# A graph-attention kernel: its set-up's key products in 13 bursts over six PSUM banks

## The chip, the core and the metric

The kernel runs on one core of a Trainium2 chip. The metric is the device time of one execution in microseconds (us); lower is better. A core has a matrix engine (TensorE, PE in the profile; its weight loads are PEld), a vector engine (DVE), a scalar engine (ACT), GpSimd (POOL) and SyncE (SP, which mostly issues DMAs). Each engine works through its own list of instructions in order and waits on semaphores for the others. Matrix products land in PSUM, which has eight banks of 128 partitions by 512 f32; everything else lies in SBUF or in device memory.

## The reference

A layer of graph attention with 16 batches of N = 512 nodes and F = 512 features, 16 heads of 32 features, and only the first 20 nodes as keys. It is done in two directions `d`: the mask with 11 labels, and its transpose. In short:

```
self_feat = concat(x, where(x.sum(-1) == 0, 0, cond)) @ W_self.T + b_self
output = self_feat
for d in range(2):
    A = (mask if d == 0 else mask.swapaxes(1, 2))[:, :, :20]    # B x N x 20 x 11 labels
    kv = self_feat[:, :20]
    q = (self_feat @ Wq[d].T + bq[d]) in 16 heads;  k = (kv @ Wk[d].T + bk[d]) in 16 heads
    aff = q . k / sqrt(32)                                      # B x N x 16 x 20
    aff = where(A.sum(-1) > 0, aff, NEG) + A @ w_bias + b_bias
    w = softmax(aff, over the 20 keys)
    output += (w @ kv) @ Wout[d] + bout[d]                      # per head
return x + relu(output)
```

## The kernel before

**What is kept and what is folded.** A score q·k is linear in the node's feature vector, so the kernel never forms q. The set-up folds each key through Wq once, and a batch's scores are then products of 512-long feature vectors with these folded keys. A softmax doesn't change if the first key's score is taken from all, so 19 key differences (`ND`) are folded in place of 20 keys. In all 16 batches x 19 differences = 304 columns per direction and head, over 512 features. The loop over batches behind the set-up forms the large products from fewer ones by sums and differences of blocks (`x_sum`, `feat_sum`, `key_sum`; `product`, line 257, forms the node features by seven such products per batch).

**The set-up, line 697 on.** In its order on PE:

- Six matmuls on a block of ones (line 735), while the first loads are on their way.
- `kv_terms` (line 780): the features of the 20 key nodes of all batches, with the part from `cond`. DVE forms from them `kvD`, the 19 differences of each batch.
- `key_rows` (line 832): Wk times `kvD`, for direction d and a group of four heads, into a PSUM bank; `key_end` puts the result into SBUF as `khD`, on whose partitions lie the four heads of 32 features each.
- **The key bursts**, `keys` (line 929). They form Wq times `khD`. The contraction is over 32 features of one head, so a matmul takes only 32 rows of PE, and the four heads of a group (`hl` = 0 to 3) are issued one after the other on the four row groups and run side by side. The output has 128 features (chunk `fc`) by the run's columns. There are 16 stages (fc, hg) with two directions each. The unit of the plan is one batch's 19 columns: 20 bursts take 25 or 26 units, 475 or 494 columns for each head, and a burst that crosses the end of a direction or a stage is cut into two runs. Heads 0 and 1 go to one pair of PSUM banks (tag `s0`), heads 2 and 3 to the other (`s1`). In the trace the two pairs appear under names that end in 0 and 1, as `s_g(2, 0, 0, 0, 16)0_776`.
- After each burst its results are copied with the softmax's scale into a stage's tile `st` in SBUF: heads 0 and 1 by ACT (line 960), heads 2 and 3 by DVE (line 962), one copy per run. When a stage is full, GpSimd copies the part of batches 0 and 1 into `gg` (line 965) and SP stores the rest, 1064 KB, to device memory `g_d` (line 968), from which the main loop loads it batch by batch. Three of the four head groups take their tiles from a pool of three (`setup_g`, line 868), the last from a pool of their own (`late`); a tile is written again only when its store has landed.

**Fillers.** The four banks of `s0` and `s1` can be written again only when ACT and DVE have copied them. So that PE has work until then, other matmuls of the set-up stand between the bursts. They take turns over four rotating accumulator banks (tag `acc`, pool `ps_acc`, line 697). What stands after which burst is the string `plan` (line 990), one letter for each step from the lists at line 981:

- k: `key_rows` (before the plan's first entry); m: `bias_terms`, DVE only (line 856); b: `biases`, ACT and DVE
- v and w: `values` (line 892), the 20 key nodes' features times Wout, a quarter of the contraction at a time. `value_pieces` adds the bias on DVE (line 917) and stores the blocks.
- c: `bias_scores` (line 870), the query bias's scores with the keys. ACT copies them, GpSimd adds `b_bias`, four DMAs store them to `cq_d`.
- n: `row_flags` (line 217), which nodes of x sum to something other than zero
- p: `block_product` (line 971), the seven feature products of batch 0 (line 282), each followed by ACT or DVE work that takes it from PSUM. Where a product closes its bank, 20 more columns are multiplied (line 287).

Steps without matmuls are placed by the burst's number n in the loop at line 1013. `mask_count`, `mask_mul`, `mask_sum` and `mask_spread` form the mask and the label bias of a batch's half: ACT and GpSimd multiply (lines 325, 322, 331), DVE sums (line 336), ACT spreads the sums in four copies into `both` (line 344). `row_sums` sums x over features (GpSimd, line 215), `x_sum` forms block differences (GpSimd, line 255), `load_cq` and `key_bias` read batch 0's bias scores back, `key_sum` and `blocks`/`spill` copy the keys and blocks of values, the latter by DMAs from one part of device memory to another.

**Where the set-up ends.** The main loop begins at line 1081 with `seed_a(0)`: ACT writes batch 0's bias scores into the PSUM banks `ps_a` (line 425), and PE's first score products add to them (`score_product`, line 395). They read `sf`, the node features, the last block of which comes from the last product of the set-up by a DVE addition (`joined`, line 305). `self_product` (line 665) forms the next batch's features in the loop.

```
for n, runs in enumerate(bursts):
    ...
    if n in (3, 4):
        values(*steps["v"].pop(0)[1])
    ...
    keys(runs)
    ...
    if n == 17:
        mask_sum(0, 1)
    ...
    if n == 18:
        mask_spread(0, 1)
```

Of the kernel before, what the change touches and what calls it, by code (L numbers as in the profile page):

```python
# [13 lines left out]
P = 128  # L14
# [4 lines left out]
def gat_kernel(  # L19
# [47 lines left out]
    def bank(name):  # L67
        return acc["pool"].tile([P, 512], F32, tag="acc", name=name)
# [148 lines left out]
    def row_flags(b):  # L217
        ps = bank(f"ps_nz{b}")
        for a in range(HL):
            nc.tensor.matmul(ps[bass.ts(a, R), :N], ones[:, :R], rss[b], start=True, stop=True)  # L220
        nzs[b] = load.tile([P, N], F32, tag="nz", name=f"nz{b}")
        nc.vector.tensor_scalar(nzs[b], ps[:, :N], 0.0, None, ALU.not_equal)
# [34 lines left out]
    def product(b, n):  # L257
# [13 lines left out]
        if first:  # L271
            parts[b, home] = bank(f"ps_{home}{b}")
        for i in range(2):
            for k in range(2):
                for a in range(2):
# [10 lines left out]
                    if last and i + k == 2:  # L286
                        nc.tensor.matmul(
                            to[:, 2 * HN :], lhs, x[:, k, : 512 - 2 * HN], start=False, stop=True, skip_group_check=True
                        )
# [407 lines left out]
    with tc.tile_pool(name="setup", bufs=1) as sp, tc.tile_pool(name="ps_acc", bufs=4, space=PSUM) as acc["pool"]:  # L697
# [18 lines left out]
        with tc.tile_pool(name="setup_k", bufs=1) as sk:  # L716
# [17 lines left out]
            warm = bank("ps_warm")  # L734
            for _ in range(6):
# [35 lines left out]
            load_x(1)  # L771
            load_adj(0, 1)
# [5 lines left out]
            kv_ps = [bank(f"ps_kv{fc}") for fc in range(C)]  # L778
# [32 lines left out]
            for fc in range(C):  # L811
# [11 lines left out]
                    kvD[:, fc].rearrange("p (b m) -> p b m", m=ND), each[:, :, 1:],  # L823
# [8 lines left out]
            def key_rows(d, jc, ks=range(C)):  # L832

                if ks[0] == 0 and (d, jc) not in of:
                    of[d, jc] = bank(f"ps_k{d}{jc}")
# [32 lines left out]
        with tc.tile_pool(name="setup_g", bufs=3) as sg:  # L868

            def bias_scores(d):  # L870

                ps = bank(f"ps_c{d}")
                for c in range(C):
# [5 lines left out]
                nc.scalar.copy(  # L879
                    t.rearrange("p (b m) -> p b m", m=NG)[:, :, 1:],  # L880
                    ps[:, : B * ND].rearrange("p (b m) -> p b m", m=ND),
                )
                nc.gpsimd.tensor_add(t, t, bb_sb.to_broadcast([P, BM]))
# [8 lines left out]
            def values(t, ds, k):  # L892
# [3 lines left out]
                if k == 0:  # L896
                    held[1 + t // 2] = bank(f"ps_v{t}{ds[0]}")
                ps = held[1 + t // 2]
                for i, d in enumerate(ds):
                    for a in range(rows // R):  # L900
                        nc.tensor.matmul(  # L901
                            ps[bass.ds(i * rows + a * R, R)], kvT[:, k, bass.ds(t * P + a * R, R)], wo_sb[d][:, k],
# [24 lines left out]
            nc.gpsimd.memset(stages["c"][:, :, :BM], 0.0)  # L927

            def keys(runs):


                pairs = [ps_s.tile([P, 2, 512], F32, tag=f"s{i}", name=f"ps_g{runs[0]}{i}", bufs=1) for i in range(2)]
                at = 0
                for fc, hg, d, lo, hi in runs:
                    n = (hi - lo) * ND
                    for hl in range(HL):
                        r = bass.ts(hl, DH)
                        nc.tensor.matmul(
                            pairs[hl // 2][:, hl % 2, at : at + n], wq_sb[r, d, hg, bass.ts(fc, P)],
                            khD[r, d * C + hg, lo * ND : hi * ND], start=at == 0, stop=True, skip_group_check=True,  # L940
                        )
                    at += n
                if not units and runs is bursts[-1]:
                    for hl in range(HL):
                        r = bass.ts(hl, DH)
                        nc.tensor.matmul(
                            pairs[hl // 2][:, hl % 2, at:], wq_sb[r, 0, 0, :P], khD[r, 0, : 512 - at],
                            start=False, stop=True, skip_group_check=True,
                        )
                at = 0  # L950
                for fc, hg, d, lo, hi in runs:
                    n = (hi - lo) * ND
                    if (fc, hg) not in stages:
                        stages[fc, hg] = (late if hg == C - 1 else sg).tile([P, B, HL, 2, ND], F32, tag="st", name=f"st{fc}{hg}")
                    st = stages[fc, hg]
                    for half in range(2):
                        to = st[:, lo:hi, bass.ts(half, 2), d].rearrange("p b h m -> p h b m")
                        of = pairs[half][:, :, at : at + n].rearrange("p h (b m) -> p h b m", m=ND)
                        if half == 0:
                            nc.scalar.activation(to, of, AF.Copy, scale=SCALE)  # L960
                        else:
                            nc.vector.tensor_scalar(to, of, SCALE, None, ALU.mult)  # L962
                    at += n
                    if d == 1 and hi == B:
# [25 lines left out]
            plan = "mmvv bvv vvc vvc vvn vvw vw vw wn p p p p p p p".split()  # L990

            units = [(fc, hg, d, b) for fc in range(C) for hg in range(C) for d in range(2) for b in range(B)]
            bursts = []
            while units:
                runs = []
                for fc, hg, d, b in units[: 25 + (len(bursts) % 5 < 3)]:
                    if runs and runs[-1][:3] == (fc, hg, d):
                        runs[-1] = (*runs[-1][:4], b + 1)
                    else:
                        runs.append((fc, hg, d, b, b + 1))  # L1000
                del units[: 25 + (len(bursts) % 5 < 3)]
# [429 lines left out]
```

## Time and profile before

| | us |
|---|---|
| median of 3 runs | 547.41 (547.02 to 547.68) |
| profiled execution, device time | 547.86 |
| its span in the trace | 546.2 |
| PE busy | 539.7 (99%) |
| DVE busy | 482.4 (88%) |
| GpSimd busy | 451.0 (83%) |
| ACT busy | 404.5 (74%) |

All times in a profile are of the one profiled execution; its device time is the span and 1.66 us that lie around it. A row of a group reads: line, engine, operation, output<-inputs, then shapes (partitions x elements), count, busy time, mean duration in ns of one, and behind the second bar the idle time of the engine just ahead of these instructions with what ended it. A row of the order of instructions reads: start and duration in us, engine, line, operation, tiles, shape, count, and in brackets the idle time ahead. A row of stretches reads: from:to and length in us; then for PE, PEld, DVE, ACT and GpSimd the busy time and the instructions; the granted clock of PE as a share of full speed; the busy share of the DMA engines; GB/s.

### The profile page before, as it was taken

How to read it: one execution, taken by the hardware profiler on the slowest of the kernel's cores; microseconds unless marked ns; L12 is line 12 of the kernel's file. 1: busy time of each engine (PE TensorE's matmuls, PEld its weight loads, DVE VectorE, ACT ScalarE, POOL GpSimd, SP SyncE). 2: the span in 40 equal slices, each digit the busy share in tenths (PEclk: the TensorE clock that was granted, in tenths of full speed). 3: DMA queues.
4: the chain of work that ended last, by engine and by line, in shares of the span. 5: the costliest groups of instructions: out<-in, count | busy, mean ns of one | idle time of the engine just before them, and what ended most of it. 6: DMA issues, size and time to landing. Idle time of an engine off the chain costs nothing.

```text
span 546.2 us, 19842 instructions
## 1 busy us (share of the span) xinstructions
PE 539.7 (99%) x8012; PEld 421.6 (77%) x8012; DVE 482.4 (88%) x716; ACT 404.5 (74%) x1000; POOL 451.0 (83%) x454
## 2 busy tenths in 40 slices
PE   9999999999999999999999999999999999999996
PEld 5544368889888878787888878887878788878784
DVE  1786678889999999999989999999999999999997
ACT  1225436898887979888888888887878787978564
POOL 2557996779989797979898989898998979797675
PEclk9999999999999999999999999999999999999998
DMA  8998799656766867777766757575766676736025
GB/s 298 377 400 324 260 365 352 235 172 183 233 218 182 226 204 210 234 213 231 209 219 186 244 174 246 179 235 179 222 212 203 203 216 189 234 93 192 1 65 194
DMA packets 94603, 120.30 MB, mean 220 GB/s; under 512 B 19201, under 2 KB 62783, under 8 KB 92465
## 3 DMA queue, kind: packets, MB, share of 16 engines
q1 hardware_dynamic: 93088, 116.69, 66.6%
q0 software_dynamic: 992, 1.57, 1.4%
q8 instruction: 63, 1.03, 0.8%
q10 hardware_dynamic: 432, 0.79, 0.4%
q14 instruction: 28, 0.22, 0.1%
HBM read 83.41 MB, written 36.90 MB: 220 GB/s over the span
## 4 chain that ended last, share of the span: by engine, by line
PE 89%; DMA 4%; DVE 3%; SPq 1%; ACT 1%; issue 0%; POOL 0%; DVEq 0%; POOLq 0%; ACTq 0%
PE ps_f L665 32%; PE ps_a L395 24%; PE ps_c L395 11%; PE ps_d L395 6%; PE ps_o_f L567 5%; PE ps_v L901 2%; DMA wk<-in_wkT 2%; DMA wo<-in_woT 1%; PE ps_a L282 1%; PE ps_o_c L567 1%; DMA xkv<-in_xkvT 1%; PE ps_l L395 1%; DVE bqt L856 1%; PE ps_c L282 1%; DVE st L962 1%
## 5 line engine op out<-in xcount | busy, mean ns | idle before, releaser
L325 ACT ACTIVATE prod<-adj,wb_sb 128x80 f32<-128x80 int32 x330 | 116.1, 430 | 0.0
L535 POOL TENSOR_TENSOR w<-w,sm 128x640 f32<-128x640 f32 x63 | 80.2, 1273 | 30.5 <-DVE sm L531 28.7
L665 PE MATMUL ps_f<-t,ws_s 128*64 128x246 f32 x720 | 80.0, 370 | 0.0
L665 PEld LDWEIGHTS ps_f<-t,ws_s 128*64 128x64 f32 x720 | 51.7, 136 | 18.9
L526 ACT ACTIVATE w<-w 128x640 f32<-128x640 f32 x60 | 43.9, 731 | 17.9 <-DVE w L522 17.9
L543 DVE STREAM_TRANSPOSE wt<-w 128x640 f32<-128x640 f32 x63 | 52.5, 833 | 0.1
L665 PE MATMUL ps_f<-x,ws_v 128*64 128x246 f32 x480 | 52.4, 371 | 0.0
L530 DVE TENSOR_REDUCE sm<-w 128x32 f32<-128x640 f32 x63 | 51.1, 811 | 1.1 <-ACT w L526 0.9
L521 DVE TENSOR_REDUCE ps_d<-w 128x32 f32<-128x640 f32 x59 | 48.7, 826 | 1.8 <-ACT ps_d L429 0.2
L522 DVE TENSOR_TENSOR w<-w,ps_d 128x640 f32<-128x640 f32 x59 | 48.4, 820 | 2.0
L665 PEld LDWEIGHTS ps_f<-x,ws_v 128*64 128x64 f32 x480 | 34.7, 137 | 13.0
L368 POOL TENSOR_TENSOR k<-gg,k 128x608 f32<-128x608 f32 x30 | 44.6, 1487 | 0.0
L395 PEld LDWEIGHTS ps_a<-gg,sf 128*64 128x64 f32 x544 | 34.2, 137 | 5.9 <-issue 5.8
L395 PE MATMUL ps_a<-gg,sf 128*64 128x152 f32 x544 | 38.6, 295 | 0.0
L395 PE MATMUL ps_d<-gg,sf 128*64 128x152 f32 x544 | 37.9, 293 | 0.0
L336 DVE TENSOR_REDUCE add<-prod 128x80 f32<-128x960 f32 x32 | 36.7, 1146 | 0.2 <-POOL prod L331 0.2
L344 ACT COPY both<-add 64x80 f32<-64x80 f32 x128 | 32.6, 255 | 5.7 <-DVE add L336 4.6
L567 PE MATMUL ps_o_c<-wt,ve 32*32 32x256 f32 (+1 forms) x480 | 35.9, 386 | 0.0
L680 POOL TENSOR_TENSOR t<-x,t 128x492 f32<-128x492 f32 x30 | 34.9, 1162 | 1.2
L395 PEld LDWEIGHTS ps_d<-gg,sf 128*64 128x64 f32 x544 | 35.3, 137 | 0.2 <-ACT sf L683 0.2
L680 POOL TENSOR_TENSOR t<-x 128x492 f32<-128x492 f32 x30 | 34.5, 1149 | 0.0
L197 ACT ACTIVATE xn<-xn 128x512 f32<-128x512 f32 x56 | 34.5, 619 | 0.0
(310 smaller groups left out, 1490.9 us busy)
## 6 DMA issues: line engine op xcount, KB each, us to landing
g_d<-st SPq DMA_DIRECT2D x16, 1064.0 KB, 8.5
gg<-g_d SPq DMA_DIRECT2D x56, 304.0 KB, 3.1
out_T<-o SPq DMA_DIRECT2D x60, 256.0 KB, 2.8
x<-in_xT SPq DMA_DIRECT2D x56, 256.0 KB, 4.1
xn<-in_xn SPq DMA_DIRECT2D x48, 256.0 KB, 3.8
adj<-in_adj SPq DMA_DIRECT2D x52, 220.0 KB, 2.9
nz<-nz_d SPq DMA_DIRECT2D x14, 256.0 KB, 4.5
adj<-in_adj SPq DMA_DIRECT2D x6, 440.0 KB, 7.7
```

Source lines behind the costliest of these rows:

```text
L325: nc.scalar.activation(p[:, :, l], a[:, :, l], AF.Identity, scale=wb_sb[:, l : l + 1])
L368: done["ksum"] = engine.tensor_sub(to, one, two)
L395: nc.tensor.matmul(slot(g)[bass.ts(p, P // 2), : HL * S].rearrange("p (h m) -> p h m", m=NG)[:, :, 1:], of(k)[:, bass.ds(first + g * P // ...
L521: nc.vector.tensor_reduce(mx, f, AX.X, ALU.max)
L522: done["weigh"] = (engine or nc.vector).tensor_sub(f, f, mx.unsqueeze(2).to_broadcast([P, per, NG]))
L526: done["exp"] = nc.scalar.activation(t, t, AF.Exp)
L530: nc.vector.tensor_reduce(sm, heads(weighs[b, c, l]), AX.X, ALU.add)
L535: done["normal"] = nc.gpsimd.tensor_mul(f, f, smalls.pop((b, c, l)).unsqueeze(2).to_broadcast([P, per, NG]))
L543: done["turn"] = nc.vector.transpose(wts[b][:, c, l], weighs.pop((b, c, l)).rearrange("p g w -> p (g w)"))
L567: nc.tensor.matmul(outsum[b][a][bass.ds(at // 2 * DH, n * DH), bass.ds(c * N // 2 + lo * R, (hi - lo) * R)].rearrange("p (n r) -> p n r", ...
L665: nc.tensor.matmul(parts[b][n in (2, 3, 5)][bass.ts(a, P // 2), bass.ts(i, HN)], lhs, x[:, k], start=False, stop=k == 1, skip_group_check= ...
L680: done["xsum"] = nc.gpsimd.tensor_sub(to, one, two)
```

## The change

Only the set-up changes, and one thing in the main loop.

**Banks.** The four rotating banks become two fixed ones, `acc0` and `acc1`, which each filler names, and one tile of two banks, `t2`. The tile holds two of the four key-feature banks at the start and, in each burst, `both`: room for a second set of runs of all four heads, 256 columns each. So a burst has six banks in place of four.

**Bursts.** The columns of `khD` now lie difference by difference (16 batches each) in place of batch by batch, so the unit is 16 columns. Thirteen bursts take for each head 30 to 32 units in the head's own bank (480 to 512 columns) and 16 or 11 units in the shared tile (256 or 176 columns), 656 to 768 in all; no run is below 96 columns. Heads 0 and 2 (even) do their shared runs first, heads 1 and 3 (odd) last. The two heads of a shared bank clear it only once (`start` only for the even one), so an odd head's shared run waits, by a PE `nop` on a semaphore, for the even head's last shared matmul.

**Copies.** ACT copies the shared runs of all four heads, and the own runs of the even heads; DVE copies the own runs of the odd heads. In PSUM a batch's differences now lie 16 elements apart.

**Fillers.** `plan` is new, and it holds the key rows as well (k). `row_flags` and `values` use 64 columns of PE in place of 32, in two matmuls for four. Of the products, only numbers 3 and 4 multiply the 20 closing columns. ACT adds `b_bias` as it copies the bias scores; GpSimd fills the tile with `b_bias` beforehand, and its two additions go.

**Order.** There are four warming matmuls in place of six. The loads of x(1) and of the mask's second half of batch 0 are issued after bursts 1 and 2, no longer before the key features. The steps placed by n move: among others row sums of batch 1, x differences and key sums stand after bursts 7 to 10, and the sum and the spreading of the mask's second half of batch 0, which stood after bursts 17 and 18 of 20, now stand after burst 12, the last, behind its two products. Of the value blocks, 12 copies of which were issued before the loop (half by GpSimd, half by SP), SP now issues one after each of bursts 8 to 11 and two after burst 12; six more are issued at three places of batch 0 in the main loop.

```diff
-    def bank(name):
-        return acc["pool"].tile([P, 512], F32, tag="acc", name=name)
+    def bank(name, i):
+        return acc["pool"].tile([P, 512], F32, tag=f"acc{i}", name=name)
...
-                    if last and i + k == 2:
+                    if n in (3, 4) and i + k == 2:
...
-            warm = bank("ps_warm")
-            for _ in range(6):
+            extra = acc["pool"].tile([P, 2, 512], F32, tag="t2", name="ps_kv")
+            warm = extra[:, 1]
+            for _ in range(4):
...
-            load_x(1)
-            load_adj(0, 1)
...
-                    held[1 + t // 2] = bank(f"ps_v{t}{ds[0]}")
+                    held[1 + t // 2] = bank(f"ps_v{t}{ds[0]}", int((t, ds) == (0, (1,))))
...
+            def keys(n):
+
+                runs = bursts[n]
+                pairs = [ps_s.tile([P, 2, 512], F32, tag=f"s{i}", name=f"ps_g{n}{i}", bufs=1) for i in range(2)]
+                both = acc["pool"].tile([P, 2, 512], F32, tag="t2", name=f"ps_g{n}2")
+                each = [sorted(runs, key=lambda run: hl % 2 == run[5]) for hl in range(HL)]
+                gone = [0] * HL
+                while any(each):
+                    hl = min((hl for hl in range(HL) if each[hl]), key=lambda hl: gone[hl])
+                    fc, hg, d, lo, hi, more, at = each[hl].pop(0)
+                    r, w = bass.ts(hl, DH), (hi - lo) * B
+                    gone[hl] += w
+                    if more:
+                        to = both[:, hl // 2, bass.ds(hl % 2 * 256 + at, w)]
+                        if hl % 2 and at == 0:
+                            behind(nc.tensor.nop(), done["key", hl - 1])
+                    else:
+                        to = pairs[hl % 2][:, hl // 2, bass.ds(at, w)]
+                    one = nc.tensor.matmul(
+                        to, wq_sb[r, d, hg, bass.ts(fc, P)], khD[r, d * C + hg, lo * B : hi * B],
+                        start=at == 0 and not (more and hl % 2), stop=True, skip_group_check=True,
+                    )
+                    if more:
+                        done["key", hl] = one
...
+                for *key, more, at in sorted(runs, key=lambda run: -run[5]):
+                    to, w = stage(*key), key[4] - key[3]
+                    if more:
+                        nc.scalar.activation(to, columns(shared, at, w), AF.Copy, scale=SCALE)
+                    else:
+                        nc.vector.tensor_scalar(to[:, 1::2], columns(pairs[1], at, w), SCALE, None, ALU.mult)
+                        nc.scalar.activation(to[:, ::2], columns(pairs[0], at, w), AF.Copy, scale=SCALE)
...
-            plan = "mmvv bvv vvc vvc vvn vvw vw vw wn p p p p p p p".split()
+            plan = "kmmk kmmmk mmmvvv vvv vvvb cvvv vvvc vnw www np pp pp pp".split()
...
+            for own_n, both_n, swap in [(30, 16, 0), (30, 11, 0), (30, 16, 1)] + [(31, 16, 0), (32, 16, 1)] * 5:
...
+                keys(n)
+                if n == 1:
+                    load_x(1)
+                if n == 2:
+                    load_adj(0, 1)
+                if n == 5:
                     mask_count(0, 0)
+                if n == 9:
                     mask_count(0, 1)
-                if n == 17:
-                    mask_sum(0, 1)
...
+                if n == 3:
+                    mask_mul(0, 0)
+                if n == 5:
+                    copies = blocks(0)
+                if n == 6:
                     mask_sum(0, 0)
-                if n == 9:
                     row_sums(1)
-                if n > 13:
-                    spill(1, nc.gpsimd)
+                if 7 < n < 12:
                     spill(1)
-                if n == 11:
+                if n == 8:
                     mask_mul(0, 1)
                     new_self(0)
...
+                if 6 < n < 9:
+                    mask_spread(0, 0, (2 * n - 14, 2 * n - 13))
+                if n == 10:
+                    load_cq(0)
                     gs.update((b, gg[:, b]) for b in range(2))
                     key_sum(0, 1)
                     load_adj(1, 0)
-                if n == 18:
+                if n == 12:
+                    mask_sum(0, 1)
                     mask_spread(0, 1)
                     key_bias(0)
                     load_adj(1, 1)
                     load_cq(1)
+                    spill(2)
```

More of the change, by code (lines that the diff above doesn't have):

```diff
@@ L217, in row_flags @@
     def row_flags(b):
-        ps = bank(f"ps_nz{b}")
-        for a in range(HL):
-            nc.tensor.matmul(ps[bass.ts(a, R), :N], ones[:, :R], rss[b], start=True, stop=True)
+        ps = bank(f"ps_nz{b}", 1)
+        for a in range(2):
+            nc.tensor.matmul(ps[bass.ts(a, P // 2), :N], ones[:, : P // 2], rss[b], start=True, stop=True)
         nzs[b] = load.tile([P, N], F32, tag="nz", name=f"nz{b}")
@@ L271, in product @@
         if first:
-            parts[b, home] = bank(f"ps_{home}{b}")
+            parts[b, home] = bank(f"ps_{home}{b}", int(home != "a"))
         for i in range(2):
@@ L693, in self_lift @@
             )
-    with tc.tile_pool(name="setup", bufs=1) as sp, tc.tile_pool(name="ps_acc", bufs=4, space=PSUM) as acc["pool"]:
+    with tc.tile_pool(name="setup", bufs=1) as sp, tc.tile_pool(name="ps_acc", bufs=1, space=PSUM) as acc["pool"]:
         wq_sb = sp.tile([P, 2, C, F], F32, name="wq_sb")
@@ L777, in gat_kernel @@
                 nc.gpsimd.tensor_add(rsk, rsk, xkv[:, k])
-            kv_ps = [bank(f"ps_kv{fc}") for fc in range(C)]
+            kv_ps = [*(bank(f"ps_kv{fc}", fc) for fc in range(2)), extra[:, 0], extra[:, 1]]
             def kv_terms(fc, k, w=R):
@@ L834, in key_rows @@
                 if ks[0] == 0 and (d, jc) not in of:
-                    of[d, jc] = bank(f"ps_k{d}{jc}")
+                    of[d, jc] = bank(f"ps_k{d}{jc}", d)
                 ps = of[d, jc]
@@ L870, in bias_scores @@
             def bias_scores(d):
-                ps = bank(f"ps_c{d}")
+                ps = bank(f"ps_c{d}", 1)
                 for c in range(C):
@@ L926, in gat_kernel @@
             stages = {"c": load.tile([P, 2, F], F32, tag="xn", name="c")}
[L927 to L952, printed above, removed]
@@ new lines, in gat_kernel, with stage @@
+            for d in range(2):
+                nc.gpsimd.tensor_copy(stages["c"][:, d, :BM], bb_sb.to_broadcast([P, BM]))
+            def keys(n):
[21 more added lines that the diff above has]
+                        done["key", hl] = one
+                def stage(fc, hg, d, lo, hi):
@@ L963, in keys, with columns @@
-                    at += n
-                    if d == 1 and hi == B:
+                    return stages[fc, hg][:, :, :, d, lo:hi].rearrange("p b h m -> p h b m")
+                def columns(t, at, n):
+                    return t[:, :, bass.ds(at, n * B)].rearrange("p h (m b) -> p h b m", b=B)
+                for *key, _, _ in runs:
+                    stage(*key)
+                shared = both.rearrange("p c (u w) -> p (c u) w", u=2)
+                for *key, more, at in sorted(runs, key=lambda run: -run[5]):
[5 more added lines that the diff above has]
+                        nc.scalar.activation(to[:, ::2], columns(pairs[0], at, w), AF.Copy, scale=SCALE)
@@ L965, in keys @@
+                for fc, hg, d, lo, hi, *_ in runs:
+                    if d == 1 and hi == ND:
+                        st = stages[fc, hg]
                         nc.gpsimd.tensor_copy(
@@ L1012, in gat_kernel @@
             del rest[:4]
-            for n, runs in enumerate(bursts):
-                for i in range(len(rest)):
-                    if (i < 1 and n > 0) or any(fc == 0 and (d, hg) == rest[0] for fc, hg, d, _, _ in runs):
-                        key_rows(*rest.pop(0))
-                if n in (3, 4):
-                    values(*steps["v"].pop(0)[1])
+            for n in range(len(bursts)):
                 if n == 0:
@@ L1030, in gat_kernel @@
[L1030 to L1040 removed]
+                for kind in plan[n]:
+                    f, args = (key_rows, rest.pop(0)) if kind == "k" else steps[kind].pop(0)
```

87 lines of the change are left out of this document (28 added, 59 removed).

## The prediction

> **What bounds the kernel now.** I read the page first, then busy time by stretches, the order of PE's instructions in the setup, and last the few instructions of ACT and DVE on which PE waits where the setup ends.
>
> ```profile
> span 546.2 us, 19842 instructions
> ...
> PE 539.7 (99%) x8012; PEld 421.6 (77%) x8012; DVE 482.4 (88%) x716; ACT 404.5 (74%) x1000; POOL 451.0 (83%) x454
> ...
> PE 89%; DMA 4%; DVE 3%; SPq 1%; ACT 1%; issue 0%; POOL 0%; DVEq 0%; POOLq 0%; ACTq 0%
> ```
>
> PE is busy all the time and carries the chain. Cut where the first key burst starts (24.25) and where the first score product starts (89.86):
>
> ```profile
> 24.25:89.86 65.61, 65.23 (x841) 33.84 (x837) 47.65 (x92) 28.00 (x67) 47.57 (x64) 1.00 0.94 336
> 89.86:118.20 28.34, 28.34 (x371) 24.47 (x368) 24.94 (x30) 22.14 (x58) 23.17 (x20) 1.00 0.66 222
> ```
>
> The bursts and their fillers last 65.61 us, with PE busy in 65.23. So the change is worth what it takes from PE's own list in this stretch, less what it makes PE wait. DMA engines are at 0.94 there too, so landings have to be looked at.
>
> **Part 1: PE's list.** A burst is 32-row matmuls on four row groups at once; fillers are 128-row matmuls on column tiles. The differences of the starts are what things cost. Every f32 matmul has two records.
>
> ```profile
> 25.30 2.25 PE L839 MATMUL ps_k<-kvD,wk 128*32 128x304 f32 x32
> 27.48 0.37 PE L938 MATMUL _g(0, 0, 1, 10, 16)0_411<-khD,wq_sb 32*128 32x114 f32 x2
> ...
> 57.55 2.78 PE L901 MATMUL ps_v<-wo,kvT 128*32 128x512 f32 x24
> 60.27 0.53 PE L938 MATMUL s_g(2, 0, 0, 0, 16)0_776<-khD,wq_sb 32*128 32x304 f32 x2
> ...
> 60.62 0.42 PE L938 MATMUL s_g(2, 0, 0, 0, 16)0_776<-khD,wq_sb 32*128 32x304 f32 x2
> ...
> 61.31 1.92 PE L901 MATMUL ps_v<-wo,kvT 128*32 128x512 f32 x16
> 63.16 0.37 PE L938 MATMUL _g(2, 0, 1, 10, 16)0_805<-khD,wq_sb 32*128 32x114 f32 x2
> ...
> 64.29 1.92 PE L901 MATMUL ps_v<-wo,kvT 128*32 128x512 f32 x16
> ```
> ```profile
> 76.03 1.88 PE L282 MATMUL ps_a<-t,ws_s 128*64 128x246 f32 x16
> 77.84 0.37 PE L938 MATMUL _g(3, 0, 1, 10, 16)0_979<-khD,wq_sb 32*128 32x114 f32 x2
> ```
> ```profile
> 94.21 3.32 PE ps_f L665 x32
> ```
>
> Rate: 32 records in pairs of 246 columns take 3.32 us, 0.8435 ns per column pass. Three values take 60.27 - 57.55 = 2.72, two take 63.16 - 61.31 = 1.85: 0.87 for each and 0.11 for the group. A key row step takes 27.48 - 25.30 = 2.18, so 2.07 without the group's 0.11. A block product takes 1.81 alone and 1.66 in a run (half of 3.32). The burst at 60.27 has 494 columns and lasts 1.04; 494 x 2 x 0.8435 is 0.83, so a burst has a fixed 0.21. The burst at 63.16, also 494, has a run of 76 columns and lasts 1.13: 0.045 more for each of its two passes, so a pass costs at least some 0.11, whatever its width.
>
> The new list: the same 9728 columns, 16.41; 13 fixed parts, 2.73; runs of 96 (five bursts) and 112 columns (five) lie under the floor by 0.03 and 0.015 a pass, 0.45; 20 values 17.4; 4 key rows 8.3; 7 products 11.6; two last closings with 20 columns 0.3; 2 bias scores (608 column passes) 1.0; 2 row flags at a value's price 1.7; 13 groups at 0.11 to 0.15, 1.6. Sum 61.5 to 61.6, so **4.0 less** than 65.61. More than half of it is seven switches fewer (7 x 0.32 = 2.2); the rest is short runs, two waits, 37 filling columns and one closing. That values and row flags use 64 columns for 32 changes no column pass: nothing.
>
> Each odd row group now waits, in PE's own queue, for the even one that shares its bank. Behind this wait stand all later matmuls of the burst. The even one's 256 shared columns end 0.43 after the start; a record outlasts its stream by 0.16 (0.42 for 304 columns), and weights add 0.11 (0.53 against 0.42): 0.70. The odd group is busy with at least 480 own columns, 0.81. So I take nothing, and 0.1 a burst, 1.3 in all, as the upper bound. A gain from it is excluded: it only waits.
>
> Matmuls of unequal length now run side by side. That later ones on a free tile may go ahead of earlier ones is shown by the closing of ps_d, where each half's 20 columns are issued right behind that half's last 246, ahead of the other half's 246:
>
> ```profile
> L282 PE MATMUL ps_d<-x,ws_v x16: 371/371/422, 73.0 to 74.6; 128*64 128x246 f32 x16
> L287 PE MATMUL ps_d<-x,ws_v x4: 183/198/213, 74.8 to 74.8; 128*64 128x20 f32 x4
> ```
>
> The first half's 20 columns start at 74.8, after all 246s (the last at 74.6) of both halves. So tiles go at their own pace, and a burst costs its columns. [...]
>
> **Part 2: copies.**
>
> ```profile
> L960 ACT ACTIVATE st<-s_g(2, 0, 0, 0, 16)0_776 128x608 f32<-128x608 f32 x1 | 0.7, 699 | 2.8 <-POOL gg L965 2.8
> L960 ACT ACTIVATE st<-_g(2, 2, 0, 14, 16)0_883 128x76 f32<-128x76 f32 x1 | 0.2, 238 | 1.7 <-PE _g(2, 2, 0, 14, 16)1_884 L938 1.7
> ```
> ```profile
> L962 DVE TENSOR_SCALAR st<-s_g(2, 0, 0, 0, 16)1_777 128x608 f32<-128x608 f32 x1 | 0.8, 794 | 2.5 <-POOL prod L331 2.5
> L962 DVE TENSOR_SCALAR st<-_g(2, 2, 0, 14, 16)1_884 128x76 f32<-128x76 f32 x1 | 0.2, 239 | 0.5 <-PE _g(2, 2, 0, 14, 16)1_884 L938 0.5
> ```
> ```profile
> 57.66 1.04 ACT L960 ACTIVATE st<-s_g(1, 3, 0, 7, 16)0_742 128x342 f32<-128x342 f32 x2 [2.61 <-PE s_g(1, 3, 0, 7, 16)1_743 L938]
> ```
> ```profile
> 57.28 0.68 DVE L917 SCALAR_TENSOR_TENSOR v<-br_sb,ps_v 128x512 f32<-128x512 f32 x1
> ...
> 61.63 1.25 DVE L962 TENSOR_SCALAR st<-s_g(2, 0, 0, 0, 16)1_777 128x608 f32<-128x608 f32 x2 [2.55 <-POOL prod L331]
> ```
>
> ACT costs 0.87 ns an element and starts 0.1 after the filler (57.66 against 57.55). It now copies some 2016 elements a burst (all shared columns and half of the others): 2.1 to 2.2 us, where it had about 1.1; DVE still 1.25. PE comes back to the even rows' own banks after the shortest gap, 2.72, and 0.43 of shared columns: 3.15. So 0.9 is left; copies cost PE nothing. They now read PSUM at a step of 16 elements, which no row shows; between no change and double I take no change, nearest to the rows (a rival below).
>
> With fewer banks one filler waits: after burst 7 the plan is value, flags, value. The last value needs the bank of the first, freed by DVE at 0.16 + 1.25 + 0.68 = 2.09; PE is there at 1.74. **0.35 more.** Elsewhere a burst lies between.
>
> Stage buffers: the bursts are longer, so four stages are written again about 6.2 to 6.7 us after they are complete, and their store must have landed.
>
> ```profile
> g_d<-st SPq DMA_DIRECT2D x16, 1064.0 KB, 8.5
> ```
>
> 8.5 is a median with other loads in the queue; the later loads of x1 and adj leave it emptier early. I take no wait; bound 2 us each, of which ACT's 0.9 hides a part: up to 3 in all.
>
> GpSimd's longest queue is after bursts 7 and 8: three adds, one multiplication, two differences.
>
> ```profile
> L215 POOL TENSOR_TENSOR rx<-rx,x 128x512 f32<-128x512 f32 x4 | 5.1, 1278 | 0.3
> L322 POOL TENSOR_TENSOR prod<-prod,wb_sb 128x880 f32<-128x880 f32 x2 | 4.2, 2109 | 0.0
> ...
> L255 POOL TENSOR_TENSOR t<-x,t 128x492 f32<-128x492 f32 x2 | 2.3, 1147 | 0.1
> ```
>
> 3 x 1.28 + 2.11 + 2 x 1.15 = 8.3, and some 5 of gathers, issues and waiting for the copies, against 14.7 from burst 7's end to the product that uses the second difference: covered by about 1. The six block copies moved to SyncE in batch 0 are first read in batch 1: nothing.
>
> **Part 3: the handover.** Of the old one:
>
> ```profile
> 86.05 1.06 ACT L344 COPY both<-add 64x80 f32<-64x80 f32 x4
> 88.02 1.04 ACT L960 ACTIVATE st<-_g(3, 3, 0, 7, 16)0_1098 128x342 f32<-128x342 f32 x2 [0.91 <-PE _g(3, 3, 0, 7, 16)1_1099 L946]
> 89.09 0.71 ACT L425 ACTIVATE ps_a<-cq 128x640 f32<-128x640 f32 x1
> ```
> ```profile
> 83.16 1.15 DVE L336 TENSOR_REDUCE add<-prod 128x80 f32<-128x960 f32 x1
> ...
> 89.96 0.67 DVE L305 TENSOR_TENSOR sf<-ps_c,sf 128x492 f32<-128x492 f32 x1 [0.67 <-PE ps_c L287]
> ```
> ```profile
> 87.92 1.93 PE L282 MATMUL ps_c<-x,ws_s 128*64 128x246 f32 x16
> ...
> 89.86 2.29 PE L395 MATMUL ps_a<-gg,sf 128*64 128x152 f32 x32
> ```
>
> The mask's sum and its spreading were done before the last burst; the seed (89.09 to 89.80) ended as PE came (89.86). Now mask_sum(0, 1) stands on DVE behind the join of the last product, its four copies behind it on ACT, and seed_a behind these, and PE's next matmul adds to that seed. From PE's last product: 0.10 to the join (89.96 - 89.86), 0.67, 1.15 less 0.05 of overlap, 1.06, 0.71 and 0.1 for two handovers: **3.7 more**, with nothing beside it on PE. It can hardly be less, as each step needs the one before; more, if GpSimd slows the join (bound 0.5).
>
> **Sum**, against the profiled run (547.86, span 546.2): -4.0 + 0.35 + 3.7 = +0.05, and I allow 0.2 for the two row-group waits: about 548.1. The median of the runs is 547.41, 0.45 under that run, so **547.7**. About 0.2%, 1.1 us, is what a measurement of this kernel can tell from no change.
>
> **Rivals.**
> 1. Faster: the handover is shorter than my chain, or the bursts save more. Without the 3.7 it is 544.0, half hidden 545.8. Against: all five steps are in one order on in-order queues. 0.14.
> 2. Slower: PE's clock. The start is cold:
>
> ```profile
> 1.11 2.93 PE L736 MATMUL ps_warm<-ones 128*128 128x128 f32 x12 [1.11 <-DVE ones L721]
> 4.04 7.35 PE L782 MATMUL ps_kv<-xkv,ws_v 128*64 128x320 f32 x44
> ```
> ```profile
> L782 PE MATMUL ps_kv<-xkv,ws_v 128*64 128x320 f32 x8 | 2.4, 751 | 0.0
> ```
> ```profile
> L782 PE MATMUL ps_kv<-xkv,ws_v 128*64 128x320 f32 x18 | 2.6, 432 | 0.0
> ```
>
> In 4.1 to 6.1 one kv record lasts 751 ns and 8 take 2.4 us, from 7 on 432 ns and 18 take 2.6: half speed at first. Four warming matmuls instead of six end some 0.85 us before the data (4.04), and the idle may delay full speed; the 3.7 idle at the handover may take it away. If either costs 3.4 us at half speed, 1.7 more: 549.4. It decides where the idle is not forgiven; the granted clock of 1.00 in both stretches above holds no such idle. 0.15. [...]
> 3. Stage buffers or GpSimd late: 1.5 more, 549.2. 0.08.
> 4. [...] 0.07.
> 5. The stepped PSUM read doubles ACT's elements: 3.8 a burst against 3.05 (3.15 less 0.1), 0.75 in eight gaps: 553.7. 0.06.
>
> **How the numbers follow.** The forecast (0.50) is 546.5 to 548.8. The range takes in it, rivals 2 and 3 and half of 1: 545.8 to 550.6. Faster 0.14, same 0.50, slower 0.36 (2 to 5).
>
> **What would show it.** In the new profile: first burst to last product 61.5 to 62.8 us; PE idle 3.5 to 4.2 before ps_a at L395, released by ACT's seed, with DVE's add and the copies to both just before it; burst intervals of 1.45 to 1.6; ACT's copies 2.1 a burst. I am wrong if PE idles before bursts, or if a kv record stays long after 6.5 us, or if the copies to both lie ahead of the last product.

## The result, and the profile after

The changed kernel takes 553.78 us in the median of four runs (553.56 to 555.55), the kernel before 547.47: a ratio of 1.0123 (95% interval 1.0102 to 1.0145). It is slower by 6.3 us, above the range of the prediction (545.8 to 550.6). The profiled execution, 555.55, is the longest of the four; the spans of the other three are 551.6 to 552.0, at a mean granted clock of 0.993 against its 0.991. What follows is of the longest run, and a stretch at half clock more than in the others (3.40 us at 0.50 in the rows below) would account for nearly all of that: 3.4 us at half speed cost 1.7 us and take 0.003 from the mean. Of the others no trace was kept.

The page of the changed kernel: PE is still busy 98% of the span and carries 94% of the chain.

```profile
span 553.2 us, 19640 instructions
...
PE 540.5 (98%) x7932; PEld 425.7 (77%) x7932; DVE 472.7 (85%) x694; ACT 410.4 (74%) x1003; POOL 445.1 (80%) x447
```

Cut into the same stretches as in the prediction (up to the first key burst, from there to the first score product, and on):

```profile
0.00:24.89 24.89, 22.74 (x268) 12.21 (x269) 10.22 (x23) 4.11 (x7) 12.00 (x19) 1.00 0.95 337
24.89:95.08 70.19, 64.33 (x764) 37.11 (x760) 42.41 (x73) 33.80 (x70) 46.09 (x62) 0.98 0.96 344
```

The middle stretch has 70.19 us where it had 65.61, and PE stands still for 5.86 of them (70.19 - 64.33). The order of PE's instructions shows where:

```profile
67.73 1.66 PE L946 MATMUL ps_g<-khD,wq_sb 32*128 32x112 f32 x32
71.62 1.35 PE L220 MATMUL ps_nz<-rx,ones 128*64 128x512 f32 x4 [2.22 <-POOL rx L215]
72.75 3.30 PE L282 MATMUL ps_a<-x,ws_v 128*64 128x246 f32 x16
75.98 1.63 PE L946 MATMUL ps_g<-khD,wq_sb 32*128 32x160 f32 x32
77.54 1.88 PE L282 MATMUL ps_d<-x,ws_v 128*64 128x246 f32 x16
...
91.14 0.30 PE L287 MATMUL ps_c<-x,ws_s 128*64 128x20 f32 x4
95.08 3.29 PE L395 MATMUL ps_a<-gg,sf 128*64 128x152 f32 x32 [3.65 <-ACT ps_a L425]
98.16 2.95 PE L395 MATMUL ps_d<-gg,sf 128*64 128x152 f32 x32
```

There are two waits: 2.22 us for the row sums of batch 1 (GpSimd, line 215) ahead of the second row flags, and 3.65 us for the seed (ACT, line 425) ahead of the first score product. Behind each, PE is slow: the product at 72.75 takes 3.30, the equal one at 77.54 takes 1.88; the score product at 95.08 takes 3.29, before it took 2.29. The granted clock (the number behind PE's busy time) says why:

```profile
68.90:72.30 3.40, 1.18 (x18) 1.00 1.02 417
72.30:75.70 3.40, 3.40 (x18) 0.50 1.01 377
75.70:79.10 3.40, 3.40 (x52) 1.00 0.57 154
92.80:96.20 3.40, 1.11 (x18) 1.00 0.96 299
96.20:99.60 3.40, 3.40 (x32) 0.50 0.95 258
```

After each wait PE runs at half clock for 3.4 us: in shorter stretches the clock reads 1.00 from 72.00 to 72.30, 0.51 and 0.50 from there to 75.70, and 0.97 from 75.70 to 76.00; and again 0.99 from 96.00 to 96.20, 0.50 from there to 99.60, and 0.97 from 99.60 to 99.80. At the start, where PE stands still for 0.81 us behind the four warming matmuls, the 44 key-feature records last 7.83 (7.35 before). There the granted clock of the trace reads 1.00 from 0 on, in the kernel before too, and only the records show half speed: one lasts 741 ns up to some 7.3 us (10 take 2.9 us from 5 to 7) and 432 ns from 7.6 on (18 take 2.6 from 7.6 to 9.6), where the turn was near 6.3 before.

```profile
1.11 2.08 PE L737 MATMUL ps_kv<-ones 128*128 128x128 f32 x8 [1.11 <-DVE ones L721]
4.00 7.83 PE L781 MATMUL ps_kv<-xkv,ws_v 128*64 128x320 f32 x44 [0.81 <-DMA ws_v<-in_wsT]
```

So the 7.0 us of span (553.2 against 546.2) come apart as follows, all from the profiled runs (another 0.7 us of their device times lies outside the span; why isn't known):

| | us |
|---|---|
| first burst later: 24.89 against 24.25 (0.44 of it by the end of the key features, 11.76 against 11.32) | +0.64 |
| wait for the row sums | +2.22 |
| flags and product behind it at half clock: 71.62 to 75.98 is 4.36; at full clock, in e1 below, 2.67 | +1.69 |
| wait for the seed | +3.65 |
| from the first score product to the end: 458.08 against 456.30 | +1.79 |
| PE's list and all else from first burst to first score product: 70.19 - 2.22 - 1.69 - 3.65 = 62.63 against 65.61 | -2.98 |

The change does save what it takes from PE's list, near enough. It loses more than twice that in waits that it makes itself and in what they do to the clock.

**Why the row sums are late.** GpSimd's rows around them (start, duration; in brackets its idle time), in the kernel before and then in the changed one, and the bias scores' stores in the changed one, with their times to landing:

```profile
62.95 1.27 POOL L213 TENSOR_TENSOR rx<-x 128x512 f32<-128x512 f32 x1
64.30 2.64 POOL L215 TENSOR_TENSOR rx<-rx,x 128x512 f32<-128x512 f32 x2
```
```profile
63.03 0.80 POOL L919 DMA_DIRECT2D vw_d<-v  x1
67.60 1.27 POOL L213 TENSOR_TENSOR rx<-x 128x512 f32<-128x512 f32 x1 [3.77 <-DMA g_d<-st]
68.95 2.62 POOL L215 TENSOR_TENSOR rx<-rx,x 128x512 f32<-128x512 f32 x2
```
```profile
L883 POOL DMA_DIRECT2D cq_d<-c x8: 620/624/692, 54.2 to 61.8; - x8
...
DMA to landing us min/median/max: 5.5/6.0/7.0
```

In the changed kernel GpSimd is not busy but idle ahead of them: 3.77 us. The profile names a store of a stage, but infers it from what landed at that moment. The program as built has what the instruction really waits for (before, then after; DMAHW is a semaphore of SyncE's DMAs, DMASW one of GpSimd's), and where the tiles lie in SBUF:

```
before: L213 TENSOR_TENSOR rx1<-x1 128x512 [waits DMAHW1,PE]
after:  L213 TENSOR_TENSOR rx1<-x1 128x512 [waits DMASW6,DMASW4,DMASW7,DMASW3,DMAHW5,DMASW2,DMASW1]
address     rx0      c        rx1
before      102848   106944   102848
after       94656    98752    98752
```

The row sums share two buffers with the tile `c` of the bias scores (all are of the tag `xn`). Before, the second row sums went into the buffer of the first, free once PE had read it. In the changed kernel they go into the buffer of `c`, free once all eight stores of the bias scores have landed; the last is issued at 61.8, and 61.8 + 5.5 is 67.3, close to the 67.60 at which GpSimd goes on. No line of the change says so: tiles are given buffers when the program is built.

**The wait for the seed** is the chain that was forecast, DVE's join and sum, then ACT's four copies and the seed:

```profile
91.47 0.67 DVE L305 TENSOR_TENSOR sf<-ps_c,sf 128x492 f32<-128x492 f32 x1 [0.93 <-PE ps_c L287]
92.06 1.14 DVE L336 TENSOR_REDUCE add<-prod 128x80 f32<-128x960 f32 x1
```
```profile
93.24 1.06 ACT L344 COPY both<-add 64x80 f32<-64x80 f32 x4 [3.24 <-DVE add L336]
94.32 0.71 ACT L425 ACTIVATE ps_a<-cq 128x640 f32<-128x640 f32 x1
```

### The profile page after: what moved, and what is told of

It reads as the page before. It is cut to its first block, busy times and chain, and to the rows that moved or that the text cites. A ratio compares the mean times of both kernels' runs of the same rounds, so it can differ in the third digit from the quotient of the medians.

```text
span 553.2 us, 19640 instructions
## 1 busy us (share of the span) xinstructions
PE 540.5 (98%) x7932; PEld 425.7 (77%) x7932; DVE 472.7 (85%) x694; ACT 410.4 (74%) x1003; POOL 445.1 (80%) x447
## 4 chain that ended last, share of the span: by engine, by line
PE 94%; DVE 2%; DMA 1%; ACT 1%; POOL 1%; issue 0%; DVEq 0%; POOLq 0%; ACTq 0%
PE ps_f L665 32%; PE ps_a L395 24%; PE ps_c L395 11%; PE ps_d L395 7%; PE ps_o_f L567 5%; PE ps_g L946 3%; PE ps_k L838 3%; PE ps_v L899 2%; PE ps_kv L781 2%; PE ps_a L282 2%; PE ps_o_c L567 1%; DMA g_d<-st 1%; PE ps_l L395 1%; PE ps_c L282 1%; DMA ws_v<-in_wsT 1%; POOL rx L215 0%
## 5 line engine op out<-in xcount | busy, mean ns | idle before, releaser
L967 ACT ACTIVATE st<-ps_g 128x448 f32<-128x448 f32 (+5 forms) x25 | 14.8, 642 | 36.0 <-PE ps_g L946 22.8
```

## The experiments

Theory A: each wait costs its idle time and then a stretch at half clock. Theory B: the bursts themselves are slower than worked out. Theory C: a wait costs its idle time alone. Ratios are to the kernel before, measured beside each kernel; behind them stands the 95% interval.

**e1_rx, e2_mask, e3_both: take away one wait, the other, both.**

```diff
 def row_sums(b):
-    t = rss[b] = load.tile([P, 2, F], F32, tag="xn", name=f"rx{b}")[:, 0]
+    if b == 1:                                  # e1, e3
+        t = rss[b] = sfp.tile([P, C, N], F32, tag="sf", name=f"rx{b}")[:, 0]
+    else:
+        t = rss[b] = load.tile([P, 2, F], F32, tag="xn", name=f"rx{b}")[:, 0]
...
+if n == 11:                                     # e2, e3
+    mask_sum(0, 1)
+    mask_spread(0, 1)
 if n == 12:
-    mask_sum(0, 1)
-    mask_spread(0, 1)
     key_bias(0)
```

> The changed kernel with one difference: the tile of batch 1's row sums is taken from the pool of the feature tiles, so that it does not take the buffer that the bias scores c leave. Theory A (each wait of PE costs its idle time and then a stretch at a lower clock): the 2.2 us wait before the second row flags goes, and the 1.7 us by which the flags and the product behind it were slow; about 3.9 less than the changed kernel's 553.8, so 549.9. Theory B (the bursts themselves are slower than worked out and the waits only show where the time is lost): under 1 us less, about 553. Theory C (a wait costs its idle time alone, the low clock has another cause): 2.2 less, 551.6, with the product behind the flags still at 3.3 us.

> The changed kernel with one difference: the sum and the spreading of the mask's second half of batch 0 stand after burst 11, ahead of the last two products. Theory A: the wait of 3.65 us before the first score product goes, and about 1.5 us of slow matmuls behind it; 553.8 - 5.1 = 548.7. Theory B: under 1 us less, about 553. Theory C: 3.65 less, 550.1, with the first 32 score matmuls still at 3.3 us.

> Both of these edits together. Theory A: 553.8 - 3.9 - 5.1 = 544.8, faster than the kernel before (547.5), because the new list of matmuls is then worth what was worked out less some 0.6 at the start. Theory B: about 552. Theory C: 553.8 - 2.2 - 3.65 = 547.9.

Measured: e1 552.14 (ratio 1.0081, 1.0059 to 1.0103; runs from 549.2 to 553.7), e2 549.69 (1.0054, 1.0030 to 1.0078; from 548.3 to 554.0), e3 547.23 (1.0000, 0.9991 to 1.0009). PE's rows of e1, at the flags and at the seed:

```profile
69.96 1.08 PE L223 MATMUL ps_nz<-rx,ones 128*64 128x512 f32 x4
70.87 1.83 PE L285 MATMUL ps_a<-x,ws_v 128*64 128x246 f32 x16
...
91.73 4.32 PE L398 MATMUL ps_a<-gg,sf 128*64 128x152 f32 x32 [3.64 <-ACT ps_a L428]
```

With its own buffer the row sums are in time: no wait, and the product takes 1.83 again. From the first burst to the first score product e1 has 66.21, where the changed kernel has 70.19: 3.98 less, as A has it. The time of the whole fell by 1.6 only, 2.2 short of A's 549.9. In e1's profiled run two other places were worse: the first burst came at 25.52 and the first score product took 4.32 in place of 3.29. The clock goes with the times of all ten runs: the three with a mean granted clock of 0.996 took 549.2 to 549.7, as A has it, the two with 0.993 551.9, and the five with 0.991 552.4 to 553.7. That fits none, one or two stretches at half clock from run to run of one program; the profiled run, of the last five, has two. In e2 the waits are the other way round:

```profile
73.48 1.08 PE L220 MATMUL ps_nz<-rx,ones 128*64 128x512 f32 x4 [2.88 <-POOL rx L215]
74.39 3.35 PE L282 MATMUL ps_a<-x,ws_v 128*64 128x246 f32 x16
...
93.79 2.29 PE L395 MATMUL ps_a<-gg,sf 128*64 128x152 f32 x32 [0.54 <-ACT ps_a L425]
```

Here the seed's wait is down to 0.54, the score product is back at 2.29, and the row sums still cost a wait and half clock. Its median is 1.0 above A's 548.7. B falls: with both edits the middle stretch is 63.10 long, 7.09 shorter than in the changed kernel. e3 was expected at 544.8 and has 547.2; its rows at the start show what is left:

```profile
4.46 8.78 PE L784 MATMUL ps_kv<-xkv,ws_v 128*64 128x320 f32 x44 [1.27 <-DMA ws_v<-in_wsT]
```

The key-feature records last 8.78 here, and the first burst comes at 26.30, 2.05 later than before. The two warming matmuls that were taken away are a third cost, and its size differs from run to run (e6 and e12 below).

**e4_fill: PE kept busy while it waits for the seed.** Sixteen matmuls of ones by ones stand behind the last product. (With them part of the result comes out different; why isn't shown. No other instruction is added or moved.)

```diff
+idle = acc["pool"].tile([P, 2, 512], F32, tag="t2", name="ps_idle")[:, 1]
+for _ in range(16):
+    nc.tensor.matmul(idle[:, :P], ones, ones, start=True, stop=True)
```

> The changed kernel with 16 matmuls of ones by ones (128 columns each, results unused) behind the last product of the set-up, so that PE is busy for some 3.4 of the 3.65 us in which it waits for the seed. Nothing else moves. Theory A: the wait stays, as the seed comes no earlier, but the first score products run at full speed: about 1.5 less, 552.3. Theory C: no change, 553.8, with the first 32 score matmuls at 3.3 us as before. Theory B says nothing of it but no change.

Measured: 554.06 (1.0118, 1.0098 to 1.0139), no gain. The trace has what A expects at that place:

```profile
71.29 1.08 PE L220 MATMUL ps_nz<-rx,ones 128*64 128x512 f32 x4 [1.18 <-POOL rx L215]
72.20 1.83 PE L282 MATMUL ps_a<-x,ws_v 128*64 128x246 f32 x16
...
89.79 3.84 PE L1075 MATMUL ps_idle<-ones 128*128 128x128 f32 x32
93.56 2.29 PE L395 MATMUL ps_a<-gg,sf 128*64 128x152 f32 x32
```

The score product takes 2.29 at once. But the other two costs change from run to run by more than the 1.5 us in question (here the row sums' wait was 1.18, and no half clock followed it: 1.00 from 71.40 to 74.80), so the time of this run decides nothing. The question was put again without them, in e7 and e8.

**e6_warm, e7_late, e8_late_fill: the start, and the seed's wait by itself.** e6 is e3 with six warming matmuls. e7 is e6 with the mask's sum back behind the last product. e8 is e7 with four matmuls in that wait:

```diff
-for _ in range(4):          # e6, e7, e8
+for _ in range(6):
     nc.tensor.matmul(warm[:, :P], ones, ones, start=True, stop=True)
...
+for _ in range(4):          # e8
+    nc.tensor.matmul(idle, ones, xs[0][:, 0], start=True, stop=True)
```

> The kernel with both edits (own buffer for the row sums, mask's sum ahead of the last products) and six warming matmuls in place of four. In the five traces with four, PE stands still for 0.8 to 1.3 us before the first loads land and full speed comes at 7.5 to 9.8 us; in the trace before it comes at 6.5. Theory A: the half speed in between, 1.0 to 3.3 us, costs half of that; about 1.2 less than 547.2, so 546.0, first burst near 24.3. If what stands ahead of the bursts is set by the loads: no change, 547.2, first burst at 25 to 26.

> As the last one, but with the mask's sum and spreading back behind the last product, so that the wait at the end of the set-up is the only difference. Theory A: 3.1 us more wait (3.65 against 0.54) and 1.5 to 2.6 of half speed: 546.0 + 4.6 to 5.7 = 550.6 to 551.7. Theory C: 549.1.

> The same with four matmuls of 512 columns, of ones by x, results unused, in that wait (3.5 us of PE time). The seed comes no earlier. Theory A: PE does not fall to half speed, so 1.5 to 2.6 less than the kernel without them: 549.1, and the first 32 score records take 2.29 us. Theory C: no change against it, and those records last as long with the fill as without.

Measured: e6 545.72 (0.9969, 0.9959 to 0.9978), e7 550.31 (1.0058, 1.0043 to 1.0073), e8 548.81 (1.0031, 1.0017 to 1.0045). The three rows that tell it, one of each kernel's profile:

```profile
4.17 6.14 PE L784 MATMUL ps_kv<-xkv,ws_v 128*64 128x320 f32 x44
```
```profile
90.28 3.62 PE L398 MATMUL ps_a<-gg,sf 128*64 128x152 f32 x32 [3.65 <-ACT ps_a L428]
```
```profile
91.23 2.29 PE L398 MATMUL ps_a<-gg,sf 128*64 128x152 f32 x32
```

In e6 PE goes from the warming matmuls into the key features almost without a wait (0.13 us), and their 44 records last 6.14, not 8.78; the first burst comes at 23.47. That trace is the best of its kind: with six warming matmuls the 44 records last 6.14 to 7.35 in seven traces, with four 7.83 to 9.06 in six. In e7 the seed's wait is worth 4.6 us (550.31 - 545.72), 3.1 of them idle. In e8 PE has work in the same time, useless work: the score product behind takes 2.29, where e7's takes 3.62 with a granted clock of 0.51 from 91.10 to 94.50, and the median is 1.5 us lower. That is near the 1.7 us that 3.4 us at half clock cost, but the runs of the two overlap (e8 from 547.8 to 550.7, e7 from 549.8 to 550.9), so the size is rough. C falls: it had 549.1 for e7 with no slow stretch behind the wait, and all four runs of e7 lie above that.

**e11_c, e5_before_late, e12_before_warm4: one part alone.** e11 is e6 with the row sums back in the buffer of `c`. The other two are the kernel before with one part of the change: the mask's sum and spreading behind the last product (after burst 19 of 20), and four warming matmuls.

> The version of 545.7 with the row sums' tile back in the buffer of the bias scores, the only difference. Theory A: 1.2 to 2.9 us of wait (the three sizes seen are 1.18, 2.22 and 2.88) and nothing to 1.7 of half speed: 546.9 to 550.3, middle 548.9. If the wait were covered by other work of PE: 545.7.

> The kernel before with one part of the change: the sum and the spreading of the mask's second half of batch 0 stand behind the last product. Theory A (a wait costs its idle time and then half speed): 3.65 us of wait and 1.5 to 2.6 us of slow matmuls behind it, the two sizes seen so far: 547.3 + 5.2 to 6.3 = 552.5 to 553.6. Theory C (idle time alone): 551.0. If the wait belongs to the new bursts and not to this order: no change, 547.3.

> The kernel before with four warming matmuls in place of six, the only difference. Theory A: PE stands still for about 1 us before the loads land and full speed comes 1 to 3.3 us later: 547.4 + 0.5 to 1.7, middle 548.5. If the wait is hidden behind the loads of the key features: 547.4.

Measured: e11 548.88 (1.0034, 1.0015 to 1.0054), 3.2 more than e6; e5 553.68 (1.0129, 1.0112 to 1.0145), 6.3 more than the kernel before; e12 548.89 (1.0023, 1.0013 to 1.0032), 1.4 more. e11 comes out at the expected middle, e12 0.4 above it, e5 at the upper end. In e12's trace the key-feature records last 9.06, in the kernel before 7.35. In e11's trace the wait is back, and the flags and the product behind it take 1.98 and 2.47, where e1 has 1.08 and 1.83:

```profile
71.43 1.98 PE L220 MATMUL ps_nz<-rx,ones 128*64 128x512 f32 x4 [2.36 <-POOL rx L215]
73.19 2.47 PE L282 MATMUL ps_a<-x,ws_v 128*64 128x246 f32 x16
```

e5's profiled run, at 551.55 the shortest of its five (the longest had 554.58), shows the same wait with no half clock behind it. Its mean granted clock is 0.996; a run with 0.994 took 552.73, and the three with 0.991 took 553.68 to 554.58. The granted clock is 1.00 in all of its rows around the wait:

```profile
93.28 2.29 PE L395 MATMUL ps_a<-gg,sf 128*64 128x152 f32 x32 [3.64 <-ACT ps_a L425]
```
```profile
87.80:91.20 3.40, 1.83 (x20) 1.32 (x18) 2.73 (x4) 0.97 (x2) 2.01 (x3) 1.00 1.04 420
91.20:94.60 3.40, 1.32 (x20) 1.32 (x22) 3.37 (x3) 3.07 (x8) 3.32 (x4) 1.00 1.01 383
94.60:98.00 3.40, 3.40 (x54) 3.27 (x52) 0.56 (x2) 1.85 (x5) 3.40 (x4) 1.00 1.04 394
```

**e10_warm8 and e9_seed: how far it goes.** e10 is e6 with eight warming matmuls. In e9, DVE copies the last burst's shared runs, behind its own, so that ACT comes to the seed earlier:

```diff
+last = n == len(bursts) - 1
-for *key, more, at in sorted(runs, key=lambda run: -run[5]):
+for *key, more, at in sorted(runs, key=lambda run: run[5] if last else -run[5]):
     to, w = stage(*key), key[4] - key[3]
-    if more:
+    if more and last:
+        nc.vector.tensor_scalar(to, columns(shared, at, w), SCALE, None, ALU.mult)
+    elif more:
```

> The version of 545.7 with eight warming matmuls in place of six. Theory A: PE stood still for at most 0.4 us with six, so nothing is left to gain and the loads (from 4.0 to 4.5 us on) are not held up by more than 0.4: 545.7, within 0.5. If the number of warming matmuls had an effect of its own: another 1.2 less, 544.5.

> The fastest version so far (own buffer for the row sums, mask's sum ahead of the last products, six warming matmuls; 545.7) and in the last burst DVE, not ACT, copies the shared runs, behind its own. ACT then seeds 1.1 us earlier. Theory A: the wait of 0.53 us before the first score product goes: 545.2. Rival: DVE, later by 1.3 us, holds up the last product's flags and join, and the wait moves there: 545.7 or more.

Measured: e10 546.64 (0.9980, 0.9970 to 0.9991), 0.9 more than e6 where 0.5 at most was expected. Its key features begin at 4.80 (4.17 in e6), as two more matmuls stand ahead of them, and 0.5 of that is left when DVE's last addition starts (538.63 against 538.12). The spans are 2.0 apart (544.8 and 542.8); the other 1.5 lies behind that addition, where the last stores of the output land. So most of the difference of these two runs isn't made at the start; what makes it isn't shown. e9 has 544.19 (0.9942, 0.9928 to 0.9957; runs from 544.12 to 544.28): faster than the kernel before by 3.2 us, and than the changed one by 9.6. That is 1.0 below what A expected; against e6's profiled run (544.72, the shortest of its nine) e9's (544.16) is 0.56 shorter, about the wait of 0.53. Why e6's median is 1.0 above its profiled run isn't shown, and e6 and e9 were not measured side by side.

```profile
0.00:23.54 23.54, 22.06 (x272) 12.56 (x272) 10.23 (x23) 4.11 (x7) 12.01 (x19) 1.00 0.96 344
23.54:85.90 62.36, 62.36 (x764) 36.30 (x761) 40.99 (x72) 32.95 (x68) 42.02 (x58) 1.00 1.00 359
```

PE is busy in all 62.36 us between first burst and first score product. That is the new plan without its waits: 3.25 less than the old one's 65.61. Its four runs lie within 0.2 us, where e1's ten are spread over 4.5: the waits whose price differs from run to run are gone. Part of so small a spread may be luck, as the start still varies: with six warming matmuls the key features' records are at full speed from 4.2 us on in e6 and from some 6.3 on in the kernel before, and e6's nine runs are spread over 2.1 us.

## Why the prediction was wrong, point by point

The forecast was no change, 547.7, and the kernel took 553.78. Its terms for PE's list and for the seed's wait held. Two costs were put at nothing in its sum: the wait for the row sums, which the prediction held to be covered, and half clock behind PE's waits, which it left to a rival. The measured time lies where rival 5 has it (553.7), by chance: ACT's copies did not double.

- **PE's list: right in kind, a little too good.** Forecast 61.6, and 0.35 for a bank; measured 62.36 in e9 and 62.63 in the changed kernel. The bursts are the larger part: the forecast's terms for them are 16.41, 2.73 and 0.45, in sum 19.6; the 13 intervals in e6 sum to 20.1: five of 1.59 (752 columns), five of 1.56 (768), and 1.60, 1.32 and 1.47.
- **Unequal runs side by side (rival 4, 0.07): next to nothing.** The rows of before show tiles at their own pace for column tiles alone. For row tiles e6 shows 0.08 us a burst at most: the five bursts of 752 columns, in runs of 112 to 304, take 1.59 each, where the forecast's terms give 1.51 (1.27 for the columns, 0.21 fixed, 0.03 for the short runs).
- **Row-group waits and copies (rival 5, 0.06): right to cost nearly nothing.** PE shows no idle time ahead of a burst or in one. The bursts' 0.5 above the forecast may hold some of the row-group waits, for which the prediction had 1.3 as the bound; no run takes them apart. ACT copies 608 elements at a step of 16 in 714 ns, against 684 to 699 in the old order: read in steps, the copies are 2 to 4% longer, not twice as long.

```profile
L970 ACT ACTIVATE st<-ps_g 128x608 f32<-128x608 f32 x6 | 4.3, 714 | 0.0
```

- **The value's wait for its bank: not there.** Forecast 0.35; the value after the flags takes 1.01 with the switch to the burst, against 0.98 for one value and one group.
- **The seed's wait: right.** Forecast 3.7, measured 3.65. It is the step where reading which work stands ahead of the seed on each queue gave the number.
- **GpSimd: the step that failed.** "Covered by about 1" counted GpSimd's work and its queue, and these were covered: with the row sums in a buffer of their own PE waits for GpSimd nowhere in the set-up's bursts in e3, e6 and e9. Rival 3 has a late GpSimd too, at 1.5 and 0.08, but with the stage buffers and the queue as its reasons. What was not asked is when the row sums' own tile comes free. They were moved from two bursts behind the last bias scores to one (the scores' eight stores take 5.5 to 7 us to land), and they took that tile's buffer. It cost 2.22 and 1.69 us in the profiled run, and 3.2 in e11 by itself.
- **The clock (rival 2): right in kind, mis-sized and misjudged.** It was priced at 1.7, once, at 0.15. No row of before shows the 3.4 us in that price, which was an assumption; the changed kernel shows 3.4 us at 0.50 behind each of two waits, e1 6.8 in and behind one. In the profiled run it came three times: 0.44 at the start (four warming matmuls for six cost 1.4 in e12), 1.69 behind the row sums, 1.79 behind the seed. The prediction's own sign, a key-feature record that stays long after 6.5 us, was there. The forecast itself put 3.7 us of idle time into PE's stream, so that a slow stretch behind it belonged to the forecast, not to a rival beside it. And the rivals were taken one at a time, while the row sums' wait brought a slow stretch with it in three of four traces (the changed kernel, e2 and e11; not e4).

With 3.65 in place of 3.7 and 62.63 for the list, the forecast would still have been no change (62.63 + 3.65 against 65.61: 0.67 more). What lies beyond it in the profiled run is the row sums, half clock and the later start, 2.22 + 1.69 + 1.79 + 0.64 = 6.34.

## What to carry to other kernels

When steps are moved on a queue, ask of each not only what it waits for to read but what it must wait for to write: whose buffer its tile takes, and when the last DMA that reads that buffer lands. Where PE was busy all the time here, waits of 1.18 to 3.65 us cost that time and, behind it, none to two stretches of 3.4 us at half clock, 1.7 us each: price the second part as well as the first. A few useless matmuls in the gap gave 1.5 us back (e8 against e7). Look at the spread of the runs and at their mean granted clock as well: e1's ten runs are spread over 4.5 us, with mean clocks from 0.991 to 0.996, and e9's four, without these waits, over 0.2.

## What the runs showed of the hardware

Waits of PE of 2.22, 2.36 and 2.88 us were followed by half clock. In the changed kernel it reads 0.50 from 72.30 to 75.70; in e11 the flags and the product behind the wait take 1.98 and 2.47, in e2 1.08 and 3.35, where e1 without that wait has 1.08 and 1.83. Waits of 1.18 and 0.54 us were not (e4: 1.08 and 1.83 behind it; e2: 2.29 for the score product). Waits of 3.64 and 3.65 us were followed by half clock for one stretch of 3.4 us in the changed kernel and e7 (0.50 from 96.20 to 99.60, 0.51 from 91.10 to 94.50), for two in e1 (0.50 from 90.10 to 96.90, from 1.6 us before the wait's end on), and by none in e5 (1.00 from 87.80 to 98.00). The rows of e1's clock:

```profile
86.70:90.10 3.40, 1.39 (x18) 1.14 (x13) 2.48 (x5) 0.21 (x1) 3.37 (x4) 1.00 1.05 405
90.10:93.50 3.40, 1.77 (x14) 1.67 (x16) 2.02 (x2) 3.00 (x8) 3.35 (x3) 0.50 1.00 414
93.50:96.90 3.40, 3.40 (x32) 3.18 (x30) 0.00 (x0) 0.80 (x2) 2.97 (x3) 0.50 0.99 301
```

In the 3.40 us ahead of the steps to half clock PE stood still for 2.22 and 2.29 us in the changed kernel (3.40 - 1.18 and 3.40 - 1.11) and for 2.01 in e1 (3.40 - 1.39). Why nearly equal waits have different prices, and what wait is short enough to cost its idle time alone, isn't shown.
